# GpSimd adds the logits, one wide sigmoid per direction, 128-row edge products: one change in a four-layer graph network

## The chip, the cores and the metric

The kernel runs on one core of a Trainium2 chip. The core has five engines that work side by side and synchronise by semaphores: TensorE (PE; PEld is its weight load), VectorE (DVE), ScalarE (ACT), GpSimd (POOL) and SyncE (SP, which here only issues DMAs). Each engine takes its instructions in the order of its own queue. The metric is the device time in microseconds (us); the kernel before has a median of 1986.42 us over three runs (1980.94 to 1987.89).

## The reference, cut to what matters

Four graph layers follow one another, each with a residual and a layer norm; `x` is 4096 x 128, `adj` a symmetric 4096 x 4096 matrix of zeros and ones. Only the first layer is touched by the change. It is a hyperbolic graph convolution:

```python
mv = proj(mobius_matvec(weight, x))
h = proj(mobius_add(mv, hyp_bias))
x_tangent = logmap0(h)
x_local = jax.vmap(lambda xi: logmap(xi, h))(h)          # 4096 x 4096 x 128
logits = (x_tangent @ wl)[:, None] + (x_tangent @ wr)[None, :] + att_b[0]
adj_att = adj * jax.nn.sigmoid(logits)
support_t = jnp.einsum('ij,ijd->id', adj_att, x_local)
h_agg = proj(expmap(h, support_t))
out = proj(expmap0(proj_tan0(h_agg)))
```

`logmap(xi, h)` depends on a pair of nodes only through their distance, a number per pair, and through the two vectors. So a 4096 x 4096 matrix of weights is enough: for each pair a function of the distance, times the edge, times the sigmoid of a sum of two scalars, one of the row node and one of the column node. The function of the distance is symmetric in the pair; the sigmoid is not, since the logit of (i, j) takes `wl` from i and `wr` from j, and that of (j, i) the reverse.

## The kernel before, in words

The nodes are cut into eight tiles of S = 512, and `Fast.pair_loop` (L1756) walks over the 36 pairs (I, J) of tiles with I <= J. For a pair it makes a block of 512 x 512 values, held as 128 partitions x 4 x 512, once for both directions; eight pairs are diagonal (I = J) and have one direction. The pieces of a pair's work are small functions with these names:

- `load` fetches the block of `adj` (SP, 1 MB); `rows` broadcasts the row of logit parts over the partitions (`di` for I, `dj` for J, SP); `edges` fetches four short rows for the distance (`el` for J, `er` for I, two 4 KB DMAs each, POOL's queue).
- `distance` (PE, four a pair) forms the product of node vectors in PSUM, `pz`: a product of 128 rows (L1822, two passes) and one of four rows in float32r that adds the two edge terms (L1825). `shift` (DVE, L1831) brings `pz` to SBUF as `t`.
- `square`, `ln`, `root`, `inverse`, `log` (ACT, L1854 to L1875, 128 x 2048 each) and `add_root`, `phi`, `mask` (DVE, L1870, L1879, L1851) turn `t` into the weight of the pair without the sigmoid.
- `sigmoid` (ACT, L1839) forms the sigmoid of each direction in `w`: four activations of 128 x 512, each with the broadcast row as its input and a column of `dr` as the bias pointer, so that the sum of the two logits is formed inside the activation. Six `w` buffers rotate.
- `first` (DVE, L1883) multiplies `w0` by `t`; `turn` (PE) transposes `t` into PSUM and `second` (DVE, L1894) multiplies `w1` by it; `sum_i` and `sum_j` (PE, L1906, L1921) multiply with the node vectors `HA`; `add_j` and `add_i` (DVE) add to the result.

The logarithms and exponentials use one activation table and the sigmoid another; `logs_and_exps` and the compiler put in a table load when it has to change.

The order of all of this is written out by hand in `SHARED_ORDER`: a list of entries `name.part.place.ahead`. Three pairs make a step (`UNIT = 3`), place says which of the three, ahead how many steps early the entry runs; `step` goes through the list once a step and issues each entry to its engine. So the list gives each engine's own order, and the semaphores give the rest. At each `mask`, `narrow` also issues two DMAs on POOL's queue which copy parts of `adj` to bfloat16 (`adjb`) for later layers.

Before the loop `layer0` prepares the node vectors `HT`, `HA` and the columns (POOL squares the vectors there, L398 and L464); `rows4` holds the first edge rows, made on chip. After the loop `scaled` (L545) has POOL do some of the scalings, and the other three layers follow from about 714 us on.

Of the kernel before, what the change touches and what calls it, by code (L numbers as in the profile page):

```python
# [44 lines left out]
SHARED_ORDER = """  # L45
log.0.0.2 ln.0.1.2 shift.3.2.2 sum_i.0.2.1 sum_j.1.2.1 phi.0.0.2 edges.0.0.3 add_j.0.1.1 sum_j.0.2.1 root.0.1.2
mask.0.0.2 add_root.0.1.2 sum_i.3.2.1 turn.3.0.2 inverse.0.1.2 first.0.0.2 square.0.2.2 second.3.0.2 turn.2.0.2
ln.0.2.2 root.0.2.2 sum_i.1.2.1 second.2.0.2 turn.0.0.2 add_j.0.2.1 load.0.2.2 add_i.0.2.1 distance.1.0.3
log.0.1.2 sum_i.0.0.2 add_root.0.2.2 turn.1.0.2 distance.2.0.3 rows.0.1.2 add_j.1.2.1 second.0.0.2 shift.1.0.3
second.1.0.2 distance.3.0.3 rows.0.2.2 phi.0.1.2 sum_j.0.0.2 sum_i.3.0.2 distance.0.0.3 mask.0.1.2 sum_i.1.0.2  # L50
edges.0.1.3 inverse.0.2.2 shift.2.0.3 turn.1.1.2 sum_i.2.0.2 shift.3.0.3 load.0.0.3 shift.0.0.3 rows.0.0.3
turn.0.1.2 log.0.2.2 sigmoid.1.1.2 phi.0.2.2 add_i.0.0.2 sigmoid.0.1.2 sum_j.1.0.2 sigmoid.0.2.2 turn.3.1.2
second.1.1.2 turn.2.1.2 second.0.1.2 add_j.1.0.2 distance.2.1.3 distance.0.1.3 sigmoid.1.2.2 second.3.1.2
distance.1.1.3 second.2.1.2 edges.0.2.3 first.0.1.2 sigmoid.1.0.3 mask.0.2.2 sum_j.1.1.2 sigmoid.0.0.3
sum_i.0.1.2 sum_i.3.1.2 shift.2.1.3 turn.0.2.2 load.0.1.3 shift.0.1.3 turn.1.2.2 square.0.0.3 turn.2.2.2
sum_i.1.1.2 shift.1.1.3 distance.3.1.3 second.0.2.2 second.2.2.2 first.0.2.2 distance.0.2.3 second.1.2.2
ln.0.0.3 turn.3.2.2 shift.3.1.3 root.0.0.3 distance.2.2.3 add_root.0.0.3 sum_i.2.1.2 add_i.0.1.2 distance.1.2.3
inverse.0.0.3 shift.2.2.3 shift.0.2.3 distance.3.2.3 add_j.0.0.2 add_j.1.1.2 square.0.1.3 second.3.2.2
sum_j.0.1.2 shift.1.2.3 sum_i.2.2.2
"""  # L60
# [3 lines left out]
class Net:  # L64
# [257 lines left out]
    def layer0(self, x, weight, bias, att_w, att_b):  # L322
# [4 lines left out]
        with ExitStack() as ctx:  # L327
# [154 lines left out]
            for k in range(3):  # L482
                for c in range(4):
# [1175 lines left out]
class Fast(Net):  # L1659

    MARKS = 160
    waits = "tile"
    banks = 5
    EARLY = 8

# [34 lines left out]
    def compare(self, ctx, pairs, natural):  # L1700
# [26 lines left out]
        for n, (I, J, jb) in enumerate(blocks):  # L1727
# [28 lines left out]
    def pair_loop(self, HT, HA, dr, rows, adp, early, rows4):  # L1756
# [7 lines left out]
        with ExitStack() as ctx:  # L1764
# [36 lines left out]
            def edges(p, _):  # L1801
                I, J = pairs[p]
                if ("er", I) not in row:
                    row["er", I] = rows4[0]
                    if I:
                        er = row["er", I] = wk.tile([4, S], F32R, tag="er", name="er", bufs=2)
                        for k in range(2):
                            nc.gpsimd.dma_start(out=er[2 * k : 2 * k + 2, :], in_=rows[1:3, I * S : (I + 1) * S])
                if p < 2:
                    st[p]["el"] = rows4[1 + p]  # L1810
                    return
                el = st[p]["el"] = wk.tile([4, S], F32R, tag="el", name="el", bufs=3)
                for k in range(2):
                    nc.gpsimd.dma_start(
                        out=el[2 * k : 2 * k + 2, :], in_=rows[3 + k, J * S : (J + 1) * S].partition_broadcast(2)
                    )
# [17 lines left out]

            def sigmoid(p, k):
                J = sides(p)[k][1]
                w = once(p, f"w{k}", wtp, "w")
                for jb in range(4):
                    nc.scalar.activation(  # L1839
                        w[:, jb, :], st[p]["d"][k], AF.Sigmoid, bias=dr[:, 4 * J + jb : 4 * J + jb + 1]  # L1840
                    )
                tables.add("sigmoid")

# [96 lines left out]
            def add_i(p, _):  # L1940
# [667 lines left out]
```

## Time and profile before

| What | Value |
|---|---|
| Runs, median (lowest to highest) | 1986.42 us (1980.94 to 1987.89) |
| The profiled execution's own time | 1988.08 us |
| Its span, first to last instruction | 1986.2 us |
| Pair loop, from the first sigmoid table load on | about 82 to 632 us |
| Busy in 82 to 632 us: PE, DVE, ACT, POOL | 514.28, 496.19, 529.84, 85.87 us |
| Sigmoid activations in the loop | 256, of 128 x 512 |
| Table loads in the loop | 25, 1283 ns each |
| Edge products (L1825) | 144, 4 rows, 488 ns and more each |
| Granted TensorE clock, mean | 0.966 of full speed |

The page of a profile covers one execution. Busy times of DVE, ACT and POOL are what their instructions took; the ends of matmuls are modelled, so PE's cost is better read from the distance between the starts of its instructions. A line of the timeline gives start, length, engine, source line, operation, output and inputs, count and, in brackets, the idle time before it and what ended it. A line of the waits gives who waited, for whom, how long in total, how many times and the longest.

### The profile page before, as it was taken

The numbers are of one execution on the slowest core, as the hardware profiler recorded it, in microseconds if no ns is written. First come the engines' busy times: TensorE is split into PE (matmuls) and PEld (weight loads), VectorE is DVE, ScalarE is ACT, GpSimd is POOL, SyncE is SP. The second block draws the span as 40 slices with busy tenths as digits, with TensorE's granted clock in tenths as the row PEclk, the third lists the DMA queues.
The fourth block names the chain that finished last, engine by engine and source line by source line (L and its number), as shares of the span: only waits on it lengthen the run. The fifth ranks groups of instructions, "written<-read, shape, count | busy, mean of one in ns | idle before, by whom it ended". The sixth has DMA issues, their size and how long they took to land.

```text
span 1986.2 us, 29386 instructions
## 1 busy us (share of the span) xinstructions
PE 1852.3 (93%) x11478; PEld 1011.1 (51%) x11494; DVE 1730.1 (87%) x2704; ACT 1326.8 (67%) x1679; POOL 140.6 (7%) x209
## 2 busy tenths in 40 slices
PE   6869999999998699999999999999999699999997
PEld 5347676676667364343434333434343476644443
DVE  6689999899998866899999999898989798878897
ACT  5699999999997757777777777777787322210000
POOL 2311111121100401000000000000000000000000
PEclk9889999899999999999999999999999899999999
DMA  9768989899954934666666666666667799968872
GB/s 330 163 143 147 168 137 169 152 159 157 159 128 165 345 117 143 219 216 205 211 213 209 210 208 211 210 211 208 205 214 258 263 422 421 421 249 317 302 276 87
DMA packets 159173, 434.46 MB, mean 219 GB/s; under 512 B 12092, under 2 KB 54876, under 8 KB 134448
## 3 DMA queue, kind: packets, MB, share of 16 engines
q1 hardware_dynamic: 113056, 330.74, 46.0%
q0 software_dynamic: 36608, 34.10, 15.6%
q10 hardware_dynamic: 9360, 67.64, 10.4%
q8 instruction: 92, 1.51, 0.3%
q14 instruction: 57, 0.47, 0.1%
HBM read 463.81 MB, written 102.84 MB: 285 GB/s over the span
## 4 chain that ended last, share of the span: by engine, by line
PE 49%; DVE 23%; ACT 18%; DMA 5%; issue 4%; SPq 0%; POOL 0%; ACTq 0%; DVEq 0%; POOLq 0%
PE pv L2076 13%; PE pa L1588 10%; PE ps L2049 9%; DVE e L2059 7%; ACT e L2057 4%; ACT w L1839 3%; PE pa L2403 2%; PE pi L1906 2%; PE pj L1921 2%; ACT s L1862 2%; ACT y L1858 2%; PE pz L1822 2%; DVE nat L2038 2%; DMA dj<-rows 2%; ACT y L1854 2%
## 5 line engine op out<-in xcount | busy, mean ns | idle before, releaser
L2059 DVE SCALAR_TENSOR_TENSOR e<-at,e 128x2048 f32<-128x2048 bf16 x256 | 583.6, 2287 | 80.2 <-ACT e L2057 79.3
L2057 ACT ACTIVATE e<-ps 128x1024 f32<-128x1024 f32 x512 | 496.2, 1022 | 163.6 <-PE ps L2049 156.8
L2076 PE MATMUL pv<-e,VA 128*64 128x512 f32 x2048 | 498.4, 608 | 2.8 <-DVE e L2059 2.5
L2049 PE MATMUL ps<-QT,KT 32*128 32x512 f32 x4096 | 326.4, 418 | 5.8 <-ACT e L2057 4.6
L2049 PEld LDWEIGHTS ps<-QT,KT 32*128 32x128 f32 x4096 | 187.2, 183 | 231.1 <-ACT e L2057 170.4
L2076 PEld LDWEIGHTS pv<-e,VA 128*64 128x64 f32 x2048 | 125.0, 136 | 245.6 <-issue 212.3
L1588 PE MATMUL pa<-w,Y 128*128 128x512 f32 x448 | 195.3, 594 | 0.0
L1585 DVE SCALAR_TENSOR_TENSOR w<-rho,col,ring 128x512 f32<-128x512 f32 x224 | 163.0, 746 | 24.9 <-PE pa L1588 12.3
L1822 PE MATMUL pz<-HT 128*128 128x512 f32 x288 | 158.6, 633 | 17.8 <-DVE t L1831 7.8
L1906 PE MATMUL pi<-HA,w 128*128 128x129 f32 x1152 | 158.6, 288 | 9.6 <-DVE w L1883 9.6
L1906 PEld LDWEIGHTS pi<-HA,w 128*128 128x128 f32 x1152 | 145.3, 201 | 21.6 <-issue 19.9
L2403 PE MATMUL pa<-ring,Y 128*128 128x512 f32 x512 | 131.0, 411 | 8.5 <-DVE ring L2378 7.2
L1588 PEld LDWEIGHTS pa<-w,Y 128*128 128x128 f32 x448 | 83.7, 190 | 106.2 <-issue 80.2
L2029 ACT ACTIVATE nat<-nat 128x2048 f32<-128x2048 f32 x64 | 122.6, 1915 | 2.2 <-DMA nat<-in_adj_dram 2.2
L1921 PE MATMUL pj<-HA,w 128*128 128x129 f32 x896 | 118.9, 290 | 3.7 <-DVE X L1933 1.7
L1921 PEld LDWEIGHTS pj<-HA,w 128*128 128x128 f32 x896 | 111.0, 202 | 11.7 <-issue 7.0
L2403 PEld LDWEIGHTS pa<-ring,Y 128*128 128x128 f32 x512 | 97.8, 195 | 34.8 <-DVE ring L2378 9.5
L1870 DVE SCALAR_TENSOR_TENSOR t<-t,s 128x2048 f32<-128x2048 f32 x36 | 82.3, 2286 | 24.6 <-ACT s L1862 24.6
L1831 DVE TENSOR_SCALAR t<-pz 128x512 f32<-128x512 f32 x144 | 93.2, 682 | 11.5 <-PE pz L1825 11.4
L1839 ACT ACTIVATE w<-di,dr 128x512 f32<-128x512 f32 x144 | 90.6, 707 | 0.7 <-DMA di<-rows 0.6
L1894 DVE TENSOR_TENSOR w<-w,ptz 128x512 f32<-128x512 f32 x112 | 73.4, 680 | 18.4 <-PE ptz L1889 18.1
L1879 DVE TENSOR_TENSOR t<-t,y 128x2048 f32<-128x2048 f32 x36 | 82.1, 2282 | 0.9 <-ACT t L1875 0.9
(416 smaller groups left out, 2292.3 us busy)
## 6 DMA issues: line engine op xcount, KB each, us to landing
ring<-adjf SPq DMA_DIRECT2D x128, 1024.0 KB, 10.2
adjf<-in_adj_dram SPq DMA_DIRECT2D x64, 1024.0 KB, 6.8
nat<-in_adj_dram ACTq DMA_DIRECT2D x64, 1024.0 KB, 5.1
ad<-in_adj_dram SPq DMA_DIRECT2D x36, 1024.0 KB, 8.8
adjb<-in_adj_dram POOLq DMA_DIRECT2D x64, 512.0 KB, 12.3
at<-adjb SPq DMA_DIRECT2D x63, 512.0 KB, 3.5
low<-adjb SPq DMA_DIRECT2D x28, 512.0 KB, 5.8
up<-adjb SPq DMA_DIRECT2D x20, 512.0 KB, 6.7
```

The lines of the kernel that those rows point to most:

```text
L1585: nc.vector.scalar_tensor_tensor(w, rho[:, I * S : (I + 1) * S], col[:, 0, j : j + 1], at[:, jb, :], op0=ALU.max, op1=ALU.mult)
L1588: nc.tensor.matmul(pa, lhsT=F[:, j, :], rhs=w, start=False, stop=(j == NT - 1), skip_group_check=True)
L1822: nc.tensor.matmul(pz, lhsT=HT[:, j * P : (j + 1) * P], rhs=HT[:, I * S : (I + 1) * S], start=True, stop=False)
L1839: nc.scalar.activation(w[:, jb, :], st[p]["d"][k], AF.Sigmoid, bias=dr[:, 4 * J + jb : 4 * J + jb + 1])
L1906: nc.tensor.matmul(row[I, "po"][ib // 2][:, ib % 2, :], lhsT=st[p]["w0"][:, jb, ib * P : (ib + 1) * P], rhs=HA[:, 4 * J + jb, :], start=False,
L1921: nc.tensor.matmul(pj[:, a, :], lhsT=st[p]["w1"][:, ib, jb * P : (jb + 1) * P], rhs=HA[:, 4 * I + ib, :], start=(ib == 0), stop=(ib == 3),)
L2029: nc.scalar.activation(nat, nat, AF.Identity, accum_out=self.deg2[:, k, i : i + 1])
L2049: nc.tensor.matmul(ps[h // 2][:, h % 2, :], lhsT=KT[r, k, jb * P : (jb + 1) * P], rhs=QT[r, q, I * S : (I + 1) * S], start=(k == q == 0), ...
L2057: nc.scalar.activation(e[:, 2 * k : 2 * k + 2, :], ps[k], AF.Exp)
L2059: nc.vector.scalar_tensor_tensor(e, at[:, jb % 4, :].unsqueeze(1).to_broadcast([P, NH, S]), 0.0, e, op0=ALU.not_equal, op1=ALU.mult,)
L2076: nc.tensor.matmul(st["po"][h // 2][g : g + 64, :], lhsT=VA[:, o : o + 64], rhs=e[:, h, :], start=(jb == 0), stop=(jb == NT - 1), skip_gro ...
L2403: nc.tensor.matmul(st["pa"], lhsT=halves[k][:, j, :], rhs=at[:, jb, :], start=(I > 0 and j == k == 0), stop=(j == NT - 1 and k == 1), skip ...
```

## The change

The sum of the two logits moves out of the activation. A new piece, `logit`, has GpSimd add the column of `dr` to the broadcast row, four additions of 128 x 512 a direction, into the `w` buffer; `sigmoid` is then one activation of 128 x 2048 in place, without a bias pointer. The tiles for the edge rows get 128 partitions instead of four, are cleared by GpSimd once, and the DMAs still write only their first four rows: the edge product runs over 128 rows, of which 124 are zero. `el` gets four fixed buffers for three, `er` two as before. Last, the written order of the three pairs is another one.

```diff
 SHARED_ORDER = """
-log.0.0.2 ln.0.1.2 shift.3.2.2 sum_i.0.2.1 sum_j.1.2.1 phi.0.0.2 edges.0.0.3 add_j.0.1.1 sum_j.0.2.1 root.0.1.2
...
-turn.0.1.2 log.0.2.2 sigmoid.1.1.2 phi.0.2.2 add_i.0.0.2 sigmoid.0.1.2 sum_j.1.0.2 sigmoid.0.2.2 turn.3.1.2
-second.1.1.2 turn.2.1.2 second.0.1.2 add_j.1.0.2 distance.2.1.3 distance.0.1.3 sigmoid.1.2.2 second.3.1.2
...
+sigmoid.1.0.0 turn.0.0.0 load.0.1.0 second.0.0.0 square.0.2.0 second.3.0.0 rows.0.2.0 first.0.0.0 distance.1.0.1
+sum_i.2.2.-1 turn.2.0.0 ln.0.2.0 turn.1.0.0 root.0.2.0 inverse.0.1.0 second.2.0.0 log.0.1.0 add_j.0.1.-1 shift.1.0.1
+sum_j.1.2.-1 add_j.1.2.-1 distance.3.0.1 second.1.0.0 distance.2.0.1 shift.3.0.1 add_i.0.2.-1 inverse.0.2.0
+logit.0.2.0 sum_j.0.2.-1 add_root.0.2.0 distance.0.0.1 add_i.0.0.3 sum_i.0.0.0 add_j.0.2.-1 shift.2.0.1 shift.0.0.1
+edges.0.1.1 load.0.2.0 logit.1.1.0 phi.0.1.0 rows.0.0.1 log.0.2.0 sum_j.0.0.0 sum_j.1.0.0 sum_i.1.0.0 sigmoid.1.1.0
+sum_i.2.0.0 logit.1.2.0 mask.0.1.0 turn.2.1.0 turn.1.1.0 phi.0.2.0 second.2.1.0 second.1.1.0 sum_i.3.0.0 sigmoid.0.1.0
+sigmoid.0.2.0 turn.0.1.0 distance.1.1.1 sigmoid.1.2.0 turn.3.1.0 logit.0.0.1 load.0.0.1 add_j.1.0.0 sigmoid.0.0.1
+add_j.0.0.0 first.0.1.0 distance.0.1.1 second.3.1.0 second.0.1.0 square.0.0.1 edges.0.2.1 sum_i.3.1.0 shift.1.1.1
+distance.2.1.1 distance.3.1.1 mask.0.2.0 turn.3.2.0 shift.2.1.1 second.3.2.0 ln.0.0.1 rows.0.1.1 logit.1.0.1
+shift.3.1.1 sum_i.0.1.0 root.0.0.1 sum_i.1.1.0 inverse.0.0.1 shift.0.1.1 turn.2.2.0 turn.1.2.0 first.0.2.0 sum_i.2.1.0
+distance.2.2.1 second.2.2.0 square.0.1.1 second.1.2.0 turn.0.2.0 add_root.0.0.1 log.0.0.1 ln.0.1.1 add_i.0.1.0
+logit.0.1.1 distance.1.2.1 shift.2.2.1 distance.0.2.1 distance.3.2.1 shift.1.2.1 sum_j.0.1.0 edges.0.0.2 second.0.2.0
+sum_j.1.1.0 shift.0.2.1 root.0.1.1 shift.3.2.1 sum_i.0.2.0 phi.0.0.1 mask.0.0.1 sum_i.3.2.0 add_root.0.1.1 add_j.1.1.0
+sum_i.1.2.0 turn.3.0.1
 """
@@ layer0 (Fast has deep = P, Net deep = 4)
-            rows4 = [keep.tile([4, S], F32R, tag=f"rows4{k}", name=f"rows4{k}") for k in range(3)]
+            rows4 = [keep.tile([self.deep, S], F32R, tag=f"rows4{k}", name=f"rows4{k}") for k in range(3)]
+            self.clear(rows4)
...
-                self.evacuate(rows4[k], p[0:4, :, :].rearrange("p a b -> p (a b)"))
+                self.evacuate(rows4[k][0:4, :], p[0:4, :, :].rearrange("p a b -> p (a b)"))
@@ Fast
+    def clear(self, tiles):
+        for t in tiles:
+            self.nc.gpsimd.memset(t.bitcast(F32), 0.0)
@@ Fast.pair_loop
+            ers = [wk.tile([self.deep, S], F32R, tag=f"er{k}", name=f"er{k}", bufs=1) for k in range(2)]
+            els = [wk.tile([self.deep, S], F32R, tag=f"el{k}", name=f"el{k}", bufs=1) for k in range(4)]
+            self.clear(ers + els)
...
-                        er = row["er", I] = wk.tile([4, S], F32R, tag="er", name="er", bufs=2)
+                        er = row["er", I] = ers[I % len(ers)]
...
-                el = st[p]["el"] = wk.tile([4, S], F32R, tag="el", name="el", bufs=3)
+                el = st[p]["el"] = els[p % len(els)]
...
-            def sigmoid(p, k):
+            def logit(p, k):
                 J = sides(p)[k][1]
                 w = once(p, f"w{k}", wtp, "w")
                 for jb in range(4):
-                    nc.scalar.activation(
-                        w[:, jb, :], st[p]["d"][k], AF.Sigmoid, bias=dr[:, 4 * J + jb : 4 * J + jb + 1]
-                    )
+                    nc.gpsimd.tensor_scalar(
+                        w[:, jb, :], st[p]["d"][k], dr[:, 4 * J + jb : 4 * J + jb + 1], None, op0=ALU.add
+                    )
+
+            def sigmoid(p, k):
+                w = st[p][f"w{k}"]
+                nc.scalar.activation(w, w, AF.Sigmoid)
                 tables.add("sigmoid")
```

More of the change, by code (lines that the diff above doesn't have):

```diff
@@ L45 @@
 SHARED_ORDER = """
-log.0.0.2 ln.0.1.2 shift.3.2.2 sum_i.0.2.1 sum_j.1.2.1 phi.0.0.2 edges.0.0.3 add_j.0.1.1 sum_j.0.2.1 root.0.1.2
[L47 to L50, printed above, removed]
@@ L51 @@
-edges.0.1.3 inverse.0.2.2 shift.2.0.3 turn.1.1.2 sum_i.2.0.2 shift.3.0.3 load.0.0.3 shift.0.0.3 rows.0.0.3
-turn.0.1.2 log.0.2.2 sigmoid.1.1.2 phi.0.2.2 add_i.0.0.2 sigmoid.0.1.2 sum_j.1.0.2 sigmoid.0.2.2 turn.3.1.2
-second.1.1.2 turn.2.1.2 second.0.1.2 add_j.1.0.2 distance.2.1.3 distance.0.1.3 sigmoid.1.2.2 second.3.1.2
-distance.1.1.3 second.2.1.2 edges.0.2.3 first.0.1.2 sigmoid.1.0.3 mask.0.2.2 sum_j.1.1.2 sigmoid.0.0.3
-sum_i.0.1.2 sum_i.3.1.2 shift.2.1.3 turn.0.2.2 load.0.1.3 shift.0.1.3 turn.1.2.2 square.0.0.3 turn.2.2.2
@@ L56 @@
[L56 to L59, printed above, removed]
+sigmoid.1.0.0 turn.0.0.0 load.0.1.0 second.0.0.0 square.0.2.0 second.3.0.0 rows.0.2.0 first.0.0.0 distance.1.0.1
+sum_i.2.2.-1 turn.2.0.0 ln.0.2.0 turn.1.0.0 root.0.2.0 inverse.0.1.0 second.2.0.0 log.0.1.0 add_j.0.1.-1 shift.1.0.1
@@ L97 @@
     banks = 6
+    deep = 4
     def pool(self, **kw):
@@ L124, in mirror @@
     def mirror(self, ctx):
+        pass
+    def clear(self, tiles):
         pass
@@ L1663 @@
     banks = 5
+    deep = P
     EARLY = 8
@@ L1749, in compare, with clear @@
                 nc.vector.tensor_reduce(self.mark(), p, AX.X, ALU.max, apply_absolute_value=True)
+    def clear(self, tiles):
+        for t in tiles:
+            self.nc.gpsimd.memset(t.bitcast(F32), 0.0)
     def mark(self):
@@ L1949, in pair_loop @@
                 square=square, ln=ln, root=root, inverse=inverse, add_root=add_root, log=log, phi=phi, first=first,
-                turn=turn, second=second, sum_i=sum_i, sum_j=sum_j, add_j=add_j, add_i=add_i,
+                turn=turn, second=second, sum_i=sum_i, sum_j=sum_j, add_j=add_j, add_i=add_i, logit=logit,
             )
@@ L1979, in step @@
                             narrow()
-                    if len(sides(p)) == 2 or not (name in pair_only or name == "sigmoid" and k == 1):
+                    if len(sides(p)) == 2 or not (name in pair_only or name in ("logit", "sigmoid") and k == 1):
                         work[name](p, k)
```

## The prediction

> **What bounds the kernel now.** I read the layer's stage, not the page's totals: the change lies wholly in `pair_loop` of layer 0. I began with the busy time by stretch over the loop (82 to 632 us; columns: stretch, length, busy PE, PEld, DVE, ACT, POOL, clock, DMA share, GB/s).
>
> ```profile
> core 0: us, PE busy (x) PEld busy (x) DVE busy (x) ACT busy (x) POOL busy (x), PEclk, DMA share, GB/s
> 82.00:632.00 550.00, 514.28 (x2896) 362.61 (x2896) 496.19 (x467) 529.84 (x469) 85.87 (x141) 0.94 0.85 154
> ...
> 116.05:531.92 415.87, 398.45 (x2274) 283.47 (x2275) 378.11 (x360) 400.65 (x353) 73.56 (x120) 0.95 0.91 155
> ```
>
> ACT is busy 96% of the steady stretch, PE 96% (but matmul ends are modelled, so I price PE by starts below), DVE 91%. The stretch runs from one sigmoid table load to the ninth after it, so a step of three pairs takes 415.87/9 = 46.2 us, of which ACT works 44.5 and DVE 42.0. POOL works 8 us a step. The ACT timeline of one batch of sigmoids (start, length) prices them:
>
> ```profile
> 440.60 1.28 ACT L1839 ACT_TABLE_LOAD   x1
> 441.89 2.56 ACT L1839 ACTIVATE w<-dj,dr 128x512 f32<-128x512 f32 x4
> 444.36 5.00 ACT L1839 ACTIVATE w<-di,dr 128x512 f32<-128x512 f32 x8
> ...
> 456.62 1.89 ACT L1854 ACTIVATE y<-t 128x2048 f32<-128x2048 f32 x1
> 458.53 1.28 ACT L1846 ACT_TABLE_LOAD   x1
> ```
>
> From 441.89 to 456.62 24 short activations take 14.73 us, 0.614 each (0.62 to 0.63 elsewhere; I use 0.62). A wide one without a bias pointer (L1854) is followed 1.80 us later by the next in the chain. A table load costs 1.29. The loop's waits show what has room:
>
> ```profile
> POOL el L1814 <- PE pz L1825: 385.7, 30, 20.7
> ...
> DVE t L1870 <- ACT s L1862: 24.6, 13, 5.1
> ...
> DVE w L1894 <- PE ptz L1889: 18.1, 20, 5.7
> ...
> ACT w L1839 <- DMA dj<-rows: 8.6, 5, 2.9
> ```
>
> DVE waits for ACT more than for anything, ACT for almost nothing: ACT sets the step, DVE is 2.5 us behind it, POOL is empty.
>
> **What the skill says, and the trace.** "TensorEngine Tiling (Array Packing)", Key Properties: changing the tiling mode drains the array. The PE timeline agrees that a 4-row product is dear, and L2403, also float32r but with 128 rows, is cheap:
>
> ```profile
> 298.89 1.02 PE L1822 MATMUL pz<-HT 128*128 128x512 f32 x2
> 299.84 0.50 PE L1825 MATMUL pz<-er,el 4*128 4x512 f32 x1
> ...
> 1599.71 2.67 PE L2403 MATMUL pa<-ring,Y 128*128 128x512 f32 x11
> ```
>
> The two HT passes take 0.95 up to the edge product's start, against 2 x 0.436 (195.3 us / 448 for L1588): 0.08 more. The edge product holds the next start for 0.42 (297.03 to 297.45 elsewhere). L2403 starts every 2.51/11 = 0.23.
> "SBUF — State Buffer", Who interferes with whom: a DVE instruction with two SBUF inputs and a GpSimd instruction that reads SBUF exclude each other for the whole of the first. The trace agrees, in the layer's preparation:
>
> ```profile
> 48.83 1.04 POOL L464 TENSOR_TENSOR squares<-HA 128x512 f32<-128x512 f32 x1 [14.32 <-DVE HA L459]
> 48.87 1.05 DVE L501 TENSOR_TENSOR de<-de,ah 128x32 f32<-128x32 f32 x1
> ...
> 54.98 0.18 DVE L501 TENSOR_TENSOR dr<-dr,ah 128x32 f32<-128x32 f32 x1
> ...
> L545 POOL TENSOR_SCALAR part<-X,wv x12: 592/654/1022, 652.8 to 663.8; 128x128 f32<-128x128 f32 x12
> L571 DVE SCALAR_TENSOR_TENSOR w<-HA,wg,part x32: 334/344/460, 653.4 to 666.1; 128x128 f32<-128x128 f32 x32
> ```
>
> The same small DVE operation takes 1.05 under POOL's and 0.18 alone: held 0.87 us for 2 x 512 values read, 0.85 ns each. Beside POOL's one-input scale (L545) DVE's loses at most 460 - 334 = 126 ns for 128 values, 1 ns each. So POOL holds the port while it streams, not for its whole 0.6 us.
> "GPSIMD Engine Reference", Engine selection: one-input work runs roughly at line rate. No run shows it at this width.
>
> **The change, part by part** (12 steps of three pairs).
> *Sigmoids.* 256 activations of 0.62 = 158.7 us go, 64 wide ones of 1.80 = 115.2 come: -43.5 on ACT. The new order splits the sigmoids into two groups a step (one alone at the step's head, five later), so ACT's stream has 39 table loads in the loop for 25: 14 x 1.29 = +18.1. Net -25.4, 2.1 a step: ACT 44.5 to 42.4.
> *Logits.* 256 POOL additions of 128x512 with a pointer scalar, 21.3 a step. The form is not shown. Below: 0.592 (L545's least, 128 wide) plus 384 more values at the 0.857 ns of POOL's memset (3645 ns for 4256) = 0.92 us. Above: 4 x 0.592 = 2.37, if it all scales. I take 0.95, because the 1 ns of port time argues for streaming plus a fixed 0.48. A gain below nothing is excluded: it is added work. POOL's DMA issues stay: 68 x 0.51 + 14 x 0.52 + 64 x 0.75 = 90 us, 7.5 a step. With 0 to 0.66 us of waiting per addition for DVE's port (DVE is in an operation with two SBUF inputs 144 x 2.20 = 317 of 530 us; 0.6 x half of 2.20), of which I take 0.3, POOL needs 21.3 x 1.25 + 7.5 = 34 us of a step. It fits.
> *DVE's port.* Each addition can hold one of the four wide operations of a pair (L1851, L1870, L1879, L1883) for 0.43 to 0.5 us: 0 to 21.3 x 0.5 = 10.7 a step. The evacuations (L1831, L1894) read PSUM and are exempt. In the new DVE sequence 4 of 12 wide operations follow another wide one; a POOL addition that waited gets in there: 4 x 0.6 x 0.45 = 1.1; the other 8 meet a running one for about 0.06 each: 0.5. I take 1.6: DVE 42.0 to 43.6.
> *Edge products.* 144 x (0.08 + 0.42 - 0.23) = -39 us on PE, 3.2 a step. PE was not the bound, so by itself this is worth nothing; what it gives is room for late inputs. If the drain stays, 3.2 a step of PE's room is gone, and PE still fits.
> *Clearing and buffers.* Nine memsets of 0.44 on POOL. Three stand where POOL idled 9.4 us (before 20.66), six in its 8.5 idle us before 77.65: nothing. Without that cover 4 us of startup. `el` goes from three buffers to four, `er` stays at two.
> *Queues.* The el/er and adjb DMAs now stand in POOL's queue behind bursts of four additions. Before, POOL sat 385.7 us waiting for PE to release `el`, so the edges were issued long ahead; landing takes 1.7/5.0/9.0 us (least, median, most). The closest pair in the new order is the edges after the additions of logit.0.0.1: they are issued some 6 us before PE wants them, so a slow landing costs PE up to 3 us, inside its room. SP issues no new DMA; its rows now wait for POOL's additions instead of ACT's sigmoids to free `di`/`dj`.
> *The new wait.* ACT waits for POOL before each sigmoid. Of the six in a step three have ten us or more and two about five. The near one is logit.0.0.1: its `w` buffer comes free with sum_i.3.0.0 (17.4 + 0.9 us into PE's step), its sigmoid stands 26.0 us into ACT's, and, adding up each engine's own sequence at the durations above, ACT leads DVE by 3.6 us (root.0.0.1 ends at 34.8, its add_root stands at 31.2) while PE leads by 2.5 (its first turn needs the mask that ends 2.5 before DVE's step does): about 6 us for a burst of 3.8 (some 5.6 with port waits). What queues behind a late sigmoid is square, ln, root of the next pair, and add_root on DVE behind them.
> *Start.* ACT's chain sets 82 to 116 us. Its first sigmoid waits for four additions after `di` lands (82.6): 82.6 + 3.8 + 1.8, and a load of 1.3 if it isn't earlier, against its end at 86.4 now: +2 to 3 us, no cover.
>
> **Sum.** A step is now 46.2 = ACT's 44.5 + 1.7 idle. After: ACT 42.4, DVE 43.6, with 0.9 idle, since two engines that alternate and a close third cannot both be full: 44.5. (46.2 - 44.5) x 12 = -20.4, start +3: -17. The profiled execution took 1988.08 us (span 1986.2): 1971. It lay 1.7 above the median of the runs, 1986.42, against which I predict 1969.
>
> **Rivals.**
> 1. *Full relief, no port loss* (0.10). DVE's holds fall in the exempt operations; ACT still sets the step at 42.4 + 1.7: -25, start +3: 1964. For it: 8 of 12 wide operations follow a PSUM one. Against: DVE's own 42.0 leaves no room for any stall.
> 2. *The gain is eaten* (0.17). Port holds of 3 to 3.5 us a step instead of 1.6, or logit.0.0.1 late by 1.5 us each step: step 45.9 to 46.3, time about 1985. For it: L501 shows the hold is real. Against: the short hold beside L545.
> 3. *POOL becomes the bound* (0.23). One mechanism: the pointer addition costs more than POOL can carry. 21.3 t + 7.5 + 6.4 = 46.2 at t = 1.52 us; that decides. At 1.7 the step is 50.1: +47 us, about 2035; at 1.6, 2010. For it: L545 takes 0.59 for 128 values, which a steeper rate with a small fixed part would explain as well. Against: the 1 ns of port time, and L464, two inputs and 512 values in 1.04.
> 4. *The edges stay dear* is no separate case: PE has the room either way.
>
> **How the numbers follow.** Forecast 0.50, rivals 0.10, 0.17, 0.23. The forecast's own range is 1957 to 1979 (stall 0.6 to 2.4 a step). Half a per cent, 10 us, is about what the measurement can tell. Faster: 0.48 of the forecast and rival 1, 0.58; same: 0.18, rival 2 and the forecast's edge; slower: 0.24. The range takes in the full relief and POOL's case up to t = 1.6: 1950 to 2012.
>
> **What would show it.** Right: logit rows on POOL near 0.95 us; wide sigmoids 1.9; table loads 14 more; edge products with 128 rows starting the next 0.23 later; L1851/L1870/L1879/L1883's means risen from 2.28 to about 2.4; steps of 44.5. Wrong: an addition of 1.5 us or more with ACT's sigmoid waiting for POOL; the four DVE means above 2.6; or long waits of PE for el.

## The result and the profile after

| | Before | After |
|---|---|---|
| Median (lowest to highest), four runs each | 1984.37 us (1980.94 to 1987.89) | 2125.07 us (2120.33 to 2127.92) |
| Ratio, 95% interval | 1 | 1.0707 (1.0677 to 1.0736) |
| Profiled execution, its span | 1988.08, 1986.2 us | 2120.33, 2118.5 us |
| First instruction after the pair loop (DVE, `junk`) | 639.80 us | 776.92 us |

The kernel became 7.1% slower, and the whole of it is lost by the end of the pair loop: the first instruction behind it starts 137.1 us later, the span is 132.3 us longer. The prediction, 1969 us in a range to 2012, was on the wrong side. Line numbers below are those of the changed kernel: L1852 is the addition of `logit`, L1858 `sigmoid`, L1868 `mask`, L1887 `add_root`, L1896 `phi`, L1900 `first`, L1835 and L1838 the two products of `distance`, L1827 `el`.

Busy time by stretch over the loop of after (columns as in the prediction: stretch, length, busy PE, PEld, DVE, ACT, POOL, clock, DMA share, GB/s):

```profile
core 0: us, PE busy (x) PEld busy (x) DVE busy (x) ACT busy (x) POOL busy (x), PEclk, DMA share, GB/s
82.00:752.00 670.00, 502.63 (x2803) 383.77 (x2802) 502.54 (x457) 495.10 (x279) 659.66 (x401) 0.86 0.65 122
116.00:600.00 484.00, 369.49 (x2123) 287.31 (x2123) 366.48 (x331) 352.62 (x199) 481.85 (x290) 0.86 0.66 121
```

POOL is busy 481.85 of 484 us, 99.6%. ACT, which filled 96% of the steady stretch before, fills 73%, DVE 76%, PE 76%. There is one bound, and it is the engine that idled before. The waits of the stretch from 60 to 790 us say the same, one engine behind the other:

```profile
ACT w L1858 <- POOL w L1852: 167.5, 31, 8.9
DVE t L1887 <- ACT s L1879: 111.5, 12, 10.8
PE pz L1838 <- DMA el<-rows: 81.3, 13, 10.0
```

The 385.7 us that POOL waited for PE before are gone. Now ACT waits for POOL, DVE for the late ACT, and PE for edge rows whose DMA POOL issues late, because they stand behind additions in its queue. The timeline of ACT, for the batch of sigmoids of one step:

```profile
357.38 1.89 ACT L1892 ACTIVATE t<-t 128x2048 f32<-128x2048 f32 x1
359.29 1.28 ACT L1858 ACT_TABLE_LOAD   x1
366.76 5.51 ACT L1858 ACTIVATE w<-w 128x2048 f32<-128x2048 f32 x3 [6.19 <-POOL w L1852]
374.32 1.91 ACT L1858 ACTIVATE w<-w 128x2048 f32<-128x2048 f32 x1 [2.05 <-POOL w L1852]
384.58 1.91 ACT L1858 ACTIVATE w<-w 128x2048 f32<-128x2048 f32 x1 [8.35 <-POOL w L1852]
386.40 1.89 ACT L1871 ACTIVATE y<-t 128x2048 f32<-128x2048 f32 x1
```

The wide sigmoid costs what was foretold (1.91, starts 1.8 apart). Between the table load and the square, 5 x 1.8 us of work take 26 us. POOL's timeline over the same time has no gap:

```profile
343.62 9.38 POOL L1852 TENSOR_SCALAR w<-di,dr 128x512 f32<-128x512 f32 x4
352.95 1.11 POOL L1827 DMA_DIRECT2D el<-rows  x2
354.10 20.20 POOL L1852 TENSOR_SCALAR w<-dj,dr 128x512 f32<-128x512 f32 x8
374.24 1.57 POOL L1981 DMA_DIRECT2D adjb<-in_adj_dram  x2
375.84 8.71 POOL L1852 TENSOR_SCALAR w<-di,dr 128x512 f32<-128x512 f32 x4
```

Four additions take 8.7 to 10.1 us here. What one costs comes from two views: the line L1852 by itself (least/median/most in ns, first and last start), and the groups by busy time with the mean.

```profile
L1852 POOL TENSOR_SCALAR w<-di,dr x144: 1553/1562/4834, 85.7 to 739.0; 128x512 f32<-128x512 f32 x144
L1852 POOL TENSOR_SCALAR w<-dj,dr x112: 1554/1586/4843, 116.1 to 752.3; 128x512 f32<-128x512 f32 x112
```

```profile
L1852 POOL TENSOR_SCALAR w<-di,dr 128x512 f32<-128x512 f32 x144 | 306.1, 2137 | 13.7 <-DMA di<-rows 11.7
L1852 POOL TENSOR_SCALAR w<-dj,dr 128x512 f32<-128x512 f32 x112 | 264.9, 2380 | 4.6 <-issue 4.1
```

About half of them take 1.55 to 1.58 us, which is the addition alone; the mean is (306.1 + 264.9) / 256 = 2.23, so 0.67 us of each is waiting inside the instruction. With the DMA issues (49.3 + 37.0 + 7.7 = 94.0 us for `adjb`, `el`, `er`) POOL has 665 us of work to do in the loop, 55.4 us for each of 12 steps, where a step had taken 46.2. From the first addition at 85.7 us to the end of the last near 754 are 668 us; before, the sigmoids ran from 83.9 to about 628.

That 0.67 is DVE's port, as the Trainium skill has it in "SBUF — State Buffer", Who interferes with whom (a DVE instruction with two SBUF inputs contends with a GpSimd one that reads SBUF). The trace agrees. Three lines of the timeline of one moment, and one of a moment in which DVE runs none of its four wide operations (those with two SBUF inputs):

```profile
359.06 2.58 DVE L1868 TENSOR_TENSOR t<-t,ad 128x2048 f32<-128x2048 f32 x1
360.35 4.84 POOL L1852 TENSOR_SCALAR w<-dj,dr 128x512 f32<-128x512 f32 x1
361.56 2.28 DVE L1896 TENSOR_TENSOR t<-t,y 128x2048 f32<-128x2048 f32 x1
...
365.17 1.56 POOL L1852 TENSOR_SCALAR w<-dj,dr 128x512 f32<-128x512 f32 x1
```

The addition that starts under `mask` ends only 1.35 us after `phi`, the next wide operation, has ended. Counted over the whole trace, 89 of the 256 additions overlap no wide operation, and none of these takes more than 34 ns over the least, 1.553 us. The 100 that start while one runs lose 1.63 us each on average, 92% of all that is lost; 15 of them wait for a second wide operation too, as the one above does.

DVE's side of it, from the groups of the stretch from 60 to 800 us:

```profile
L1868 DVE TENSOR_TENSOR t<-t,ad 128x2048 f32<-128x2048 f32 x36 | 92.0, 2555 | 0.8
L1887 DVE SCALAR_TENSOR_TENSOR t<-t,s 128x2048 f32<-128x2048 f32 x36 | 87.4, 2426 | 111.5 <-ACT s L1879 111.5
L1900 DVE TENSOR_TENSOR w<-w,t 128x2048 f32<-128x2048 f32 x36 | 86.5, 2401 | 0.6 <-ACT w L1858 0.5
L1896 DVE TENSOR_TENSOR t<-t,y 128x2048 f32<-128x2048 f32 x36 | 83.9, 2331 | 0.9 <-ACT t L1892 0.9
```

They were 2282 to 2286 ns before. The excess, (2555 + 2426 + 2401 + 2331 - 4 x 2284) x 36 = 20.8 us, is 0.08 us per addition and 1.7 a step. So the two engines don't lose alike: an addition waits 0.67 us for DVE, and DVE loses 0.08. Nor is DVE's loss what costs the 137 us. An addition that comes while one of these runs has to see it to its end: they hold 350 of the 670 us, 0.52, and half of one is 1.21, together 0.63. The evacuations, which read PSUM (L1844 and L1911), take 680 and 678 ns, for 682 and 680 before.

PE's edge products are what they were meant to be. The timeline of PE:

```profile
198.12 1.02 PE L1835 MATMUL pz<-HT 128*128 128x512 f32 x2
198.58 0.80 PE L1838 MATMUL pz<-rows,el 128*128 128x512 f32 x1
199.21 1.02 PE L1835 MATMUL pz<-HT 128*128 128x512 f32 x2
```

From one `distance` to the next are 1.09 us. Before, it was 1.38 with passes of the same length (1.02):

```profile
191.59 1.02 PE L1822 MATMUL pz<-HT 128*128 128x512 f32 x2
192.54 0.50 PE L1825 MATMUL pz<-er,el 4*128 4x512 f32 x1
192.97 1.12 PE L1822 MATMUL pz<-HT 128*128 128x512 f32 x2
```

Where the two passes take 1.12, it was 1.48 to 1.49 before (91.44 to 92.93) and is 1.19 to 1.20 with the new edge products (221.58 to 222.77 in the kernel with them alone). So like compared with like, a `distance` is 0.29 us shorter, 42 us in 144. The edge product's own record grew, from 0.50 to 0.80, while the next `distance` starts sooner: the distance of starts is what counts.

Last, the start. ACT's first square begins at 93.75 us, against 86.39 before: 7.4 us later, where the prediction had 2 to 3. The row `di` lands at 85.7 us, for 82.6, and the first burst of additions takes 6.2 us, for 3.8. Some of the lateness of `di` may come from the clearing. Lines of DVE and POOL after:

```profile
9.69 2.59 DVE L1718 TENSOR_SCALAR sized<-sized 128x128 bf16<-128x128 bf16 x2
10.51 1.45 POOL L1759 MEMSET rows<- 128x512 f32 x3
22.59 1.03 POOL L402 TENSOR_TENSOR squares<-X 128x512 f32<-128x512 f32 x1 [9.95 <-issue]
```

and before:

```profile
9.72 1.19 DVE L1712 TENSOR_SCALAR sized<-sized 128x128 bf16<-128x128 bf16 x2
```

Beside the three memsets these two small operations of DVE take 2.59 us for 1.19, the copy of `wT` behind them on DVE starts at 13.19 us for 11.83, and POOL's next squares at 22.59 for 20.66. But those squares also start late, at 22.06, in the second experiment below, which clears nothing, and at 21.02 in the fifth, which clears. What the clearing costs is therefore not settled.

### The profile page after: what moved, and what is told of

Same layout as the page of the kernel before. It is cut to its first block, busy times and chain, and to the rows that moved or that the text cites. A ratio compares the mean times of both kernels' runs of the same rounds, so it can differ in the third digit from the quotient of the medians.

```text
span 2118.5 us, 29551 instructions
## 1 busy us (share of the span) xinstructions
PE 1849.7 (87%) x11494; PEld 1043.4 (49%) x11494; DVE 1753.8 (83%) x2704; ACT 1303.6 (62%) x1501; POOL 718.4 (34%) x474
## 4 chain that ended last, share of the span: by engine, by line
PE 43%; DVE 16%; ACT 10%; POOL 10%; issue 5%; DMA 4%; ACTq 0%; DVEq 0%; POOLq 0%; SPq 0%
PE pv L2093 12%; PE pa L1593 9%; POOL w L1852 9%; PE ps L2066 8%; DVE e L2076 7%; ACT e L2074 3%; DMA ring<-adjf 3%; PE pj L1938 3%; PE pa L2420 2%; DVE nat L2055 2%; PE pi L1923 2%; PE pz L1835 1%; PE pa L2438 1%; ACT nat L2046 1%; DMA el<-rows 1%
## 5 line engine op out<-in xcount | busy, mean ns | idle before, releaser
L1852 POOL TENSOR_SCALAR w<-di,dr 128x512 f32<-128x512 f32 x144 | 306.1, 2137 | 13.7 <-DMA di<-rows 11.7
L1852 POOL TENSOR_SCALAR w<-dj,dr 128x512 f32<-128x512 f32 x112 | 264.9, 2380 | 4.6 <-issue 4.1
L1858 ACT ACTIVATE w<-w 128x2048 f32<-128x2048 f32 x64 | 119.7, 1905 | 167.6 <-POOL w L1852 167.5
L1835 PE MATMUL pz<-HT 128*128 128x512 f32 x288 | 177.9, 704 | 25.8 <-DVE t L1844 24.3
L1590 DVE SCALAR_TENSOR_TENSOR w<-rho,col,ring 128x512 f32<-128x512 f32 x224 | 162.9, 746 | 25.0 <-PE pa L1593 12.3
L1887 DVE SCALAR_TENSOR_TENSOR t<-t,s 128x2048 f32<-128x2048 f32 x36 | 87.4, 2426 | 111.5 <-ACT s L1879 111.5
L1923 PE MATMUL pi<-HA,w 128*128 128x129 f32 x1152 | 154.0, 287 | 14.0 <-DVE w L1900 14.0
L1838 PE MATMUL pz<-er,el 128*128 128x512 f32 x112 | 102.4, 915 | 69.7 <-DMA el<-rows 69.7
L1593 PEld LDWEIGHTS pa<-w,Y 128*128 128x128 f32 x448 | 83.7, 190 | 106.1 <-issue 80.4
L1906 PE MATMUL ptz<-ident,t 128*128 128x128 f32 x448 | 74.7, 310 | 49.6 <-DVE t L1868 29.6
```

The costliest lines, as they stand in the source:

```text
L1590: nc.vector.scalar_tensor_tensor(w, rho[:, I * S : (I + 1) * S], col[:, 0, j : j + 1], at[:, jb, :], op0=ALU.max, op1=ALU.mult)
L1593: nc.tensor.matmul(pa, lhsT=F[:, j, :], rhs=w, start=False, stop=(j == NT - 1), skip_group_check=True)
L1835: nc.tensor.matmul(pz, lhsT=HT[:, j * P : (j + 1) * P], rhs=HT[:, I * S : (I + 1) * S], start=True, stop=False)
L1852: nc.gpsimd.tensor_scalar(w[:, jb, :], st[p]["d"][k], dr[:, 4 * J + jb : 4 * J + jb + 1], None, op0=ALU.add)
L1923: nc.tensor.matmul(row[I, "po"][ib // 2][:, ib % 2, :], lhsT=st[p]["w0"][:, jb, ib * P : (ib + 1) * P], rhs=HA[:, 4 * J + jb, :], start=False,
```

## The experiments

The theory to test, called P: POOL is the bound, since an addition costs 1.56 us plus waiting, and everything else follows from it. Its rivals: the new order or its table loads cost the time; the edge products or their DMAs do; or theory D, the hold on DVE, does. Each ratio is against the kernel before, run beside it on the same chip.

**The new order with the sums in ACT.** After, with `sigmoid` as before the change.

```diff
-                    nc.gpsimd.tensor_scalar(
-                        w[:, jb, :], st[p]["d"][k], dr[:, 4 * J + jb : 4 * J + jb + 1], None, op0=ALU.add
-                    )
...
-                w = st[p][f"w{k}"]
-                nc.scalar.activation(w, w, AF.Sigmoid)
+                w = once(p, f"w{k}", wtp, "w")
+                for jb in range(4):
+                    nc.scalar.activation(
+                        w[:, jb, :], st[p]["d"][k], AF.Sigmoid, bias=dr[:, 4 * J + jb : 4 * J + jb + 1]
+                    )
```

> The changed kernel with its new order and its 128-row edge products, but the sums of the logits formed inside ACT again (four short sigmoids a direction with the bias pointer). Theory P (POOL's additions are the bound): their queue is empty again, so the time returns to that of before, raised at most by the 14 more table loads (18 us): 1975 to 2005 us. Theory O (the new order with its split sigmoids and later edges is at fault): it stays above 2080 us. Theory D (DVE loses the port to POOL): as P.

Measured: 2002.18 us, 1.0059 (1.0038 to 1.008). Of the 7.1% 6.5 points go with POOL's additions, and POOL waits for PE again:

```profile
POOL el L1827 <- PE pz L1838: 352.0, 28, 23.2
```

So neither the order, nor the edge products, nor the 39 table loads (25 before) make the 7%; together they make 0.6%.

**The old order with the sums on POOL.** Before, four-row edges, with four additions written straight ahead of each sigmoid.

```diff
-turn.0.1.2 log.0.2.2 sigmoid.1.1.2 phi.0.2.2 add_i.0.0.2 sigmoid.0.1.2 sum_j.1.0.2 sigmoid.0.2.2 turn.3.1.2
+turn.0.1.2 log.0.2.2 logit.1.1.2 sigmoid.1.1.2 phi.0.2.2 add_i.0.0.2 logit.0.1.2 sigmoid.0.1.2 sum_j.1.0.2 logit.0.2.2 sigmoid.0.2.2 turn.3.1.2
...
```

> The kernel before with its old order and 4-row edge products; only the sums move to POOL, each direction's four additions right ahead of its sigmoid in the written order, and the sigmoid is one wide one. Theory P: POOL works 256 x 2.2 + 90 = 653 us in the loop, which lasts 550 now: 2080 to 2130 us. Theory O: ACT is relieved by 43 us and nothing else changes: 1950 to 1990 us. Theory D: DVE loses 20 us to the port, ACT gains 43: about 1980 us.

Measured: 2311.62 us, 1.162 (1.1585 to 1.1655), far above what was expected. The waits of this kernel (60 to 1000 us; L1839 is the addition, L1845 the sigmoid) tell why:

```profile
ACT w L1845 <- POOL w L1839: 377.8, 64, 8.1
...
POOL w L1839 <- DMA dj<-rows: 157.6, 7, 29.0
```

Here all 64 sigmoids wait, and POOL is not full either: five bursts stand in a row and then nothing is ready. The new order spreads the bursts and issues them earlier; given that POOL forms the sums, it is, with its edge products, worth some 185 us. It covers much of the price of the additions, and was not what cost time.

**Only the first direction on POOL.** After, with the second direction's sums in ACT: half the additions.

```diff
             def logit(p, k):
                 w = once(p, f"w{k}", wtp, "w")
+                if k == 1:
+                    return
...
+                if k == 0:
+                    nc.scalar.activation(w, w, AF.Sigmoid)
+                    return
+                for jb in range(4):
+                    nc.scalar.activation(
+                        w[:, jb, :], st[p]["d"][k], AF.Sigmoid, bias=dr[:, 4 * J + jb : 4 * J + jb + 1]
+                    )
```

> The changed kernel, but only the first direction of each pair has its sums on POOL (144 additions for 256); the second direction's sigmoid is again four short ones with the bias pointer on ACT. Theory P: POOL works 144 x 2.2 + 94 = 411 us, less than the loop's 550, so it is no longer the bound: 1975 to 2015 us. Theory O: above 2080 us. Theory D: half of 20 us of port loss is left, about 1990 us.

Measured: 1989.99 us, 1.0014 (1.0 to 1.0029), no difference from before that can be told. L1854 is the addition, L1863 the wide sigmoid:

```profile
L1854 POOL TENSOR_SCALAR w<-di,dr 128x512 f32<-128x512 f32 x144 | 395.0, 2755 | 48.1 <-PE pj L1947 20.8 <-issue 14.7 <-DMA di<-rows 12.0
L1863 ACT ACTIVATE w<-w 128x2048 f32<-128x2048 f32 x36 | 67.0, 1899 | 16.4 <-POOL w L1854 16.4
```

The 144 additions fit: 395 us of some 550. The time alone would fit theory D as well, which also had about 1990 us; the waits decide for P: ACT waits 16.4 us for POOL, of 167.5. In the shorter loop one addition's mean is 2.76, for 2.23: 80 of the 144 start under a wide operation of DVE, and 25 of these wait for a second one.

**A fifth addition in each burst.** After, with the last addition of each four made twice.

```diff
-                for jb in range(4):
+                for jb in (0, 1, 2, 3, 3):
```

> The changed kernel with one addition in four done twice (five a direction, 64 more in all, the fifth repeating the fourth): the suspected cost raised by a quarter. Theory P: each of the 64 costs the loop its whole price, 1.56 us undisturbed to 2.23 us with its waits: +100 to +143 us over the changed kernel, 2225 to 2268 us. Theory O: POOL isn't the bound, under +20 us. Theory D: 64 more holds of at most 0.45 us: under +30 us.

Measured: 2227.63 us, 1.1193 (1.1155 to 1.1231). 64 more additions cost 102.6 us (97 by the two ratios), 1.5 to 1.6 us each, which is about what one takes undisturbed: an engine that sets the time passes on what it is given. The rivals allowed under 20 and under 30 us.

**The addition with two inputs.** After, with the column of `dr` as a second input, repeated along the row, in place of a pointer.

```diff
-                    nc.gpsimd.tensor_scalar(
-                        w[:, jb, :], st[p]["d"][k], dr[:, 4 * J + jb : 4 * J + jb + 1], None, op0=ALU.add
-                    )
+                    nc.gpsimd.tensor_tensor(
+                        w[:, jb, :], st[p]["d"][k], dr[:, 4 * J + jb : 4 * J + jb + 1].to_broadcast([P, S]), ALU.add
+                    )
```

> The changed kernel with POOL's additions written as a sum of two tensors (the column of dr broadcast along the row) in place of tensor and pointer scalar; same sums. The other two-input operations of POOL take 1.04 to 1.27 us at this size against 1.56 for the pointer form. Theory P: POOL has 256 x 0.29 to 0.52 us less to do: 75 to 130 us faster than the changed kernel, 1995 to 2050 us. Theory D (the port matters): two inputs hold DVE's port for 0.87 us instead of 0.45, and the time rises above 2125 us.

Measured: 2058.59 us, 1.037 (1.0339 to 1.0402), 9 us above the range of P and far below that of D. Each of them named a part of it.

```profile
L1852 POOL TENSOR_TENSOR w<-di,dr x144: 1027/1049/3102, 87.3 to 673.1; 128x512 f32<-128x512 f32 x144
```

The two-input form takes 1.05 us where the pointer form takes 1.56. The mean falls by less, to 446.7 / 256 = 1.74, and POOL's idle time ahead of additions grows from 18.3 to 78.9 us. DVE pays: its four wide operations come to 3290, 2922, 2806 and 2744 ns, 0.37 us per addition where it was 0.08. So the time falls by 66 us, though the additions take 124 us less.

**An immediate addend.** After, with the constant 0.5 in place of the pointer; the column's logit is left out.

```diff
-                        w[:, jb, :], st[p]["d"][k], dr[:, 4 * J + jb : 4 * J + jb + 1], None, op0=ALU.add
+                        w[:, jb, :], st[p]["d"][k], 0.5, None, op0=ALU.add
```

> The changed kernel with a constant 0.5 in place of the column of dr in POOL's additions (the column's logit is left out of the sum, so the output differs): the price of the pointer operand by itself. If the pointer costs, the addition falls from 1.56 towards 1.0 us and the time by up to 140 us; if the rate of POOL's loop over the values costs, it stays at 1.5 to 1.6 us and the time at 2115 to 2130 us.

Measured: 2074.5 us (two runs), 1.0452 (1.0412 to 1.0492). The line of the first direction:

```profile
L1852 POOL TENSOR_SCALAR w<-di x144: 1477/1501/3465, 86.6 to 691.9; 128x512 f32<-128x512 f32 x144
```

The undisturbed addition stays at 1.5 us, as the second expectation said: the pointer is 0.08 us of the 1.56, and what is dear is the one-input operation with a scalar itself. But the time is 50 us below that of after, and below the 2115 to 2130 us expected. The additions take 526.7 us in all, for 571.0. The 0.08 us each is 20 us of that; for the rest, none of the 122 additions that start under a wide operation of DVE waits for a second one, where with the pointer 15 do and lose 32 us by it. Why the form makes this difference is open.

L545 took 592 ns at the least for 128 values, so 384 more cost 961: 2.50 ns a value and 0.27 us fixed (an estimate from these two). The Trainium skill, "GPSIMD Engine Reference", Engine selection, says of GpSimd that "1-input is roughly line-rate" and of two inputs that it is about twice as slow as on DVE. For two inputs the runs agree: 1049 / 512 = 2.0 ns a value, for 2284 / 2048 = 1.1 on DVE's wide operations. For one input the measurement decides: on 512 values it is the slower form of the two.

**Half of it, with two inputs.** The kernel of the third experiment with the addition of the fifth, in search of a version that beats both.

```diff
-                    nc.gpsimd.tensor_scalar(
-                        w[:, jb, :], st[p]["d"][k], dr[:, 4 * J + jb : 4 * J + jb + 1], None, op0=ALU.add
-                    )
+                    nc.gpsimd.tensor_tensor(
+                        w[:, jb, :], st[p]["d"][k], dr[:, 4 * J + jb : 4 * J + jb + 1].to_broadcast([P, S]), ALU.add
+                    )
```

> After with the sums of the first direction alone on GpSimd, as two-input additions (the column broadcast along the row); ACT forms the other direction's sums as before. e3, the same with the pointer addition, took 1990 us, with 395 us of GpSimd's time on 144 additions and ACT waiting 16 us for it. Theory P: what is left of GpSimd's price is gone with 1.0 us an undisturbed addition: ACT waits under 8 us, 1978 to 1988 us. Rival theory L: the 14 further table loads and ACT's own work set the time, e3's waits for GpSimd were covered: 1987 to 1993 us. Rival theory H: a two-input addition holds DVE's port for longer and slows DVE's wide operations: 1993 to 2010 us.

Measured: 1999.02 us, 1.0071 (1.0042 to 1.01): theory H. ACT waits 5.9 us for POOL, and yet it is slower than with the pointer form (1.0014), by some 9 us. DVE's groups show what the form takes (L1905 is `phi`, L1877 `mask`):

```profile
L1905 DVE TENSOR_TENSOR t<-t,y 128x2048 f32<-128x2048 f32 x36 | 95.2, 2645 | 0.7 <-ACT t L1901 0.5
L1877 DVE TENSOR_TENSOR t<-t,ad 128x2048 f32<-128x2048 f32 x36 | 94.7, 2631 | 0.8
```

With L1896 and L1909 (2532 and 2576) the excess is 44.9 us, 0.31 per addition; with the pointer form it was 13.6, 0.09. Here, where POOL has room, the form that is slower by itself is the better one. That the loss comes from DVE's 31 us is argued from these groups, not tested apart.

**The old order, half on POOL.** Order of before, 128-row edges, the first direction's additions written earlier in the list, and `edges.0.2.3` moved up.

```diff
-log.0.1.2 sum_i.0.0.2 add_root.0.2.2 turn.1.0.2 distance.2.0.3 rows.0.1.2 add_j.1.2.1 second.0.0.2 shift.1.0.3
+add_root.0.2.2 turn.1.0.2 distance.2.0.3 rows.0.1.2 logit.0.1.2 add_j.1.2.1 second.0.0.2 shift.1.0.3 second.1.0.2 distance.3.0.3
...
```

> The old order with its 25 table loads, 128-row edge products, and the sums of the first direction of each pair on POOL, issued some ten us or more ahead of their sigmoids (edges.0.2.3 moved ahead of the third of them). Theory P: POOL has 144 x 2.2 to 2.75 + 94 = 411 to 490 us of work, below the loop's 550, and ACT is relieved of 144 x 0.62 - 36 x 1.80 = 24 us without a new table load: 1960 to 1975 us, faster than both kernels. Theory D: DVE, 2 us behind ACT in a step, loses 1 us a step to the port: 1970 to 1980 us. If POOL's additions are late again, above 1990 us.

Measured: 2050.72 us, 1.0327 (1.0303 to 1.0352); expected was a gain, or more than 1990 us if the additions were late again. They were. POOL's work fits, but its queue runs in order, and an early addition waits in it for a `w` buffer or for its row (L1850 is the addition):

```profile
POOL w L1850 <- DMA di<-rows: 72.5, 6, 23.7
POOL w L1850 <- PE pi L1928: 67.8, 5, 16.3
```

ACT then waits 80.4 us for POOL. Writing them earlier did not make them early.

**The edge products alone.** Before, with the 128-row products, the memsets and four `el` buffers, and nothing else of the change.

```diff
-                el = st[p]["el"] = wk.tile([4, S], F32R, tag="el", name="el", bufs=3)
+                el = st[p]["el"] = els[p % len(els)]
...
```

> The kernel before with its old order and the sums inside ACT, and only the edge products over 128 rows (cleared tiles, four el buffers). A distance should start the next 1.09 us later for 1.48: 56 us less work for PE. All theories alike: PE was not the bound, so little comes of it, 1970 to 1988 us; a gain of more than 10 us would say that PE's order was on the path beside ACT.

Measured: 1995.36 us, 1.0049 (1.0032 to 1.0067): slower, though PE's `distance` is down to 1.08 to 1.09. The 56 us expected compare the longer form before with the shorter one after; like for like they are 42. In its trace row broadcasts come late (L1855 is `sigmoid`):

```profile
ACT L1855 <- DMA dj<-rows: 16.2, 5, 4.6
```

With a further 5.2 us on single sigmoids that is 21.4, where it was 8.6 before, and DVE's wait for the root behind it grew from 24.6 to 54.6. Two runs asked whether the fourth buffer, or the place of the broadcasts in SP's queue, is the reason. First, three buffers:

```diff
-            els = [wk.tile([self.deep, S], F32R, tag=f"el{k}", name=f"el{k}", bufs=1) for k in range(4)]
+            els = [wk.tile([self.deep, S], F32R, tag=f"el{k}", name=f"el{k}", bufs=1) for k in range(3)]
```

> The order and the activations of before, the 128-row edge products, and three el buffers as before in place of the fourth. e5, the same with four buffers, took 1995 us (1.0049 of before) although PE was quicker; there dj landed 12.8 us after its issue (median; 8.3 before) and ACT waited some 21 us in the loop for it. Theory D: the fourth buffer lets GpSimd issue the edge rows, and the 512 KB copies behind them in its queue, earlier, into the row broadcasts: with three buffers dj lands in 7 to 9 us again, ACT's wait falls below 10 us, and the time comes to 1975 to 1988 us. Rival theory N: the quicker edge products alone shift PE and with it the copies: dj stays at 11 us or more and the time at 1992 to 1998 us.

Measured: 1992.52 us, 1.0034 (1.0019 to 1.005). The median landing of `dj` fell to 8.7 us as theory D said, but ACT still waited 17.1 us for it and the time stayed: the fourth buffer is not the reason. Then the order on SP's queue, in the edge kernel with four buffers, and, as a control, in the kernel before:

```diff
-ln.0.2.2 root.0.2.2 sum_i.1.2.1 second.2.0.2 turn.0.0.2 add_j.0.2.1 load.0.2.2 add_i.0.2.1 distance.1.0.3
-log.0.1.2 sum_i.0.0.2 add_root.0.2.2 turn.1.0.2 distance.2.0.3 rows.0.1.2 add_j.1.2.1 second.0.0.2 shift.1.0.3
-second.1.0.2 distance.3.0.3 rows.0.2.2 phi.0.1.2 sum_j.0.0.2 sum_i.3.0.2 distance.0.0.3 mask.0.1.2 sum_i.1.0.2
+ln.0.2.2 root.0.2.2 sum_i.1.2.1 second.2.0.2 turn.0.0.2 add_j.0.2.1 rows.0.1.2 rows.0.2.2 load.0.2.2 add_i.0.2.1 distance.1.0.3
+log.0.1.2 sum_i.0.0.2 add_root.0.2.2 turn.1.0.2 distance.2.0.3 add_j.1.2.1 second.0.0.2 shift.1.0.3
+second.1.0.2 distance.3.0.3 phi.0.1.2 sum_j.0.0.2 sum_i.3.0.2 distance.0.0.3 mask.0.1.2 sum_i.1.0.2
```

> As e5 (order and activations of before, 128-row edge products, four el buffers), but the two row broadcasts of a step, rows.0.1.2 and rows.0.2.2, stand ahead of load.0.2.2 in the written order; in e5 they stand in SP's queue behind that load of 1 MB, which waits for DVE's mask. Theory R: the row broadcasts that come late are what e5 lost (ACT waited 21 us for dj, 8.6 before, and DVE behind it 54.6 for ACT, 24.6 before). Then ACT's wait for dj falls below 5 us and the time to 1972 to 1985 us. Rival theory K: the waits for dj only take the place of other idle time, and the loop is set by ACT's work and the alternation with DVE: dj's waits go and the time stays at 1988 to 1997 us.

> The kernel before with the same two row broadcasts moved ahead of load.0.2.2, and nothing else. It is the control of e11: ACT's 8.6 us of waiting for dj are all that it can save. Theory R: 1976 to 1985 us, and e11 at or below it. Rival theory K: no change, 1983 to 1989 us, with e11 above it by as much as e5 stands above before.

Measured: 1978.58 us, 0.995 (0.9931 to 0.997), with the edge products; 1986.25 us, 0.9997 (0.9985 to 1.0008), without. The first is the one version here that beats both kernels, the one before by 0.5%. Its `dj` lands within 5.2 to 7.6 us (median 5.5, for 12.8), and what is left of the wait is

```profile
ACT w L1855 <- DMA dj<-rows: 1.7, 2, 1.0
```

DVE's wait for the root falls from 54.6 to 35.2 us. From the first sigmoid's table load to the end of the loop it takes 631.30 - 88.08 = 543.2 us, for 563.4 with the broadcasts late and 557.2 in the kernel before. So theory R holds for the edge kernel: 128-row products, with the clearing and the fourth buffer, are worth some 8 us there (1986.25 to 1978.58), and behind the 1 MB load the late broadcasts took more than that. In the control R failed: there the move left ACT's wait for `dj` at 8.5 us, with a median landing of 12.3 us for 8.3, and the time stayed too. Why the quicker PE makes the broadcasts later in the one order and the move does not help in the other was not tried.

## Why the prediction was wrong

**The step that failed** is *Logits*: 0.95 us an addition, out of 0.92 to 2.37. Measured are 1.56. The lower bound took the 128-wide scale and added the other 384 values at the rate of a memset, 0.857 ns; they cost 2.50. "Because the 1 ns of port time argues for streaming" was no argument: the time for which DVE is held says nothing of how long POOL works, since the addition that takes 1.56 us alone costs DVE 0.08 on average. The memset reads nothing, and L464, two inputs in 1.04, is another form of instruction. L545 was the nearest row, and the steep reading of it, named under rival 3, was right.

**The second term, the wait for the port,** was taken as 0.3 out of 0 to 0.66, and the prediction gives no reason for staying that far below the upper end. Measured are 0.67: that end itself, DVE's share of the time times half an operation.

Both together, in the prediction's own sum: 21.3 x (1.56 + 0.67) + 7.8 = 55.3 us a step for 34. So "it fits" was wrong, and with it the step that ACT and DVE were to set. That is rival 3, in its place (POOL) and by its mechanism, past the 1.52 from which it was to decide; with a wait of 0.67 it would have decided from 1.13 us on. Its own price stopped at 1.7 with a wait of 0.3. The experiment with a fifth addition shows the bound directly, and the half with 144 additions shows that below it the time comes back.

**Right:** the wide sigmoid (1.80 foretold, 1.8 between starts); 14 more table loads; the port's toll on DVE (1.6 us a step, measured 1.7, and per addition much the same where POOL has room, 0.09 for 0.08). The gain on ACT is there too: the sigmoids take 119.7 us for 162.0 and the table loads 50.1 for 32.1, 24 us less of the 25 foretold, but no one waited for it any more. A `distance` has the length of the sum, 1.10 us foretold and 1.09 measured, and the saving of 0.27 is measured as 0.29. The records divide it otherwise: the edge product starts 0.46 us after the first pass, for 0.95 before, and the next `distance` 0.63 after it, not 0.23.

**Edges "worth nothing by itself"** was too small by some 8 us in the old order, and it needed a move of the row broadcasts to show.

**The start** is 7.4 us later for 2 to 3, mostly by the longer burst and the later row. **Clearing at nothing** is neither shown nor refuted: the squares that end POOL's gap start 1.9 us later, but they move by as much between kernels that clear alike.

**The near case, logit.0.0.1,** was the right place with the wrong size. Its sigmoid is the last of the batch shown, ahead of the square; it waits 8.35 us, for none foretold. Its burst takes 8.71 us instead of 3.8 to 5.6, and POOL comes to it late from the eight additions before it; the first sigmoid of the group of five waits 6.19 too. The lateness of `el` came as well, 81.3 us in 13 waits for the 3 us named, but from POOL's full queue and not from a slow landing: DMAs of `el` land in 2.6 us (median; 5.2 before), and with half the additions PE waits 6.0 us for them.

## What to carry to other kernels

An idle engine is cheap only at its own rate for that very form of operation. Take the price from a row with the same operation and operands, and scale it to the new width twice: once as if all of it grew with the width, once as if most of it were fixed. Where what the engine can carry lies between the two, the forecast has no side until a row or a run of that instruction decides. To the price belongs the wait for a shared port. The neighbour's busy share times half of one of its operations gave 0.63 us here for a measured 0.67; in the half kernel, where DVE's wide operations follow each other more closely, the same estimate gives about 0.7 for a measured 1.2. A written order is to be judged with the work it was written for: the one that looked like the cost covered some 185 us of it.

## What the runs showed of the hardware

- On POOL, 128 x 512 float32, undisturbed: one input and a pointer scalar 1.56 us, with an immediate 1.50, two inputs 1.05.
- On the shared port the loss is uneven and depends on the form: per addition DVE lost 0.08 to 0.09 us to the pointer form (after, and half of it) and 0.31 to 0.37 to the two-input form; POOL lost 0.45 to 1.2 us per addition in these kernels (mean less the undisturbed one). After, an addition that started under a wide operation of DVE lost 1.63 us on average, and one that met none at most 0.03.
- A float32r product of 128 rows with 124 of zeros between products of 128 makes a `distance` 0.29 us shorter, start to start (1.38 to 1.09), than one of four rows, though its own record is longer. The Trainium skill, "TensorEngine Tiling (Array Packing)", Key Properties, says that a change of tiling mode drains the array; the runs show the cost, and not that a drain is its cause.
- DVE's bf16 scale of 128 x 128 took 2.32 to 2.33 us in the six traces where it runs beside the three memsets of POOL, and 0.93 in two without them. That the memsets hold it is argued from this alone.
- The longer the loop, the lower the granted TensorE clock in it: in 116 to 520 us 0.95 before, 0.92 with two-input additions, 0.90 with the immediate, 0.85 after, 0.83 with five additions and 0.79 with the sums on POOL in the old order. After, with PE busy 76% of the stretch, the lower clock was not what cost the time; why it fell was not tested.
